# Attention in 64x64 quadrants (layers 2, 3) in place of three shared 128x1024 PSUM tiles (layer 0)

## The chip, the cores and the metric

The kernel runs on one core of a Trainium2 chip. The metric is the device time of one execution in microseconds, the median of the runs. Engines are named as the profile names them: PE (TensorE matmuls) with its weight loads (PEld), DVE (VectorE), ACT (ScalarE), POOL (GpSimd) and SP (the queue that issues most DMAs).

## What is computed

Four layers act in turn on x of shape (2, 512, 32, 32) in fp32. Layer 0 is attention on 64 sampled keys for 1024 queries, with a bias from a small MLP on every (query, key) pair, then a projection and a channel MLP. Layer 1 is a linear attention. Layers 2 and 3 are group norm, attention with 8 heads of 64 channels over 1024 positions, a projection and a residual. The parts that the change touches are these (cut from the reference):

```python
# layer 0: the bias of 16 (batch, group) units, 1024 queries x 64 keys each
bias = relu(bias @ cpb_w1 + cpb_b1)        # 2 -> 128
bias = relu(bias @ cpb_w2 + cpb_b2)        # 128 -> 128
bias = (bias @ cpb_w3 + cpb_b3)            # 128 -> 1
sim = einsum('bhid,bhjd->bhij', qh, kh) + bias
# layers 2 and 3
attn = softmax(einsum('bhcn,bhcm->bhnm', q, k) * scale)
out = einsum('bhnm,bhcm->bhcn', attn, v)
```

## The kernel before, in words

**Layer 0.** `layer0` (L99) builds, for each of 16 units u (one group of 64 channels of one image; two units are a pair), the bias of 64 keys. It does so in 16 quads per unit, written (o, jj): four keys by 1024 queries each. `first_hidden` (L368) lets DVE add a row `x` (tile `tx`) and a column `y` (tile `ty`, in PSUM) with a clamp at zero, into four tiles `h1`. `second_hidden` (L389) forms four PSUM tiles `hp` of 128x1024, for q from 0 to 3. Each takes 8 matmuls of 32 output columns (L400), four of them side by side in the four column strips of the array. ACT evacuates each `hp` with a Relu (L404) into a tile `h2`. After the first one ACT also multiplies by a sign `flip` (L411, only for q equal to 1, on the tile of q equal to 0), and POOL does the other sign (L408) and two adds (L412). `last_product` (L416) is then 8 matmuls `sim` per two quads (L427).

Weights: `last_weights` (L173) loads cpb_w3 as a row `w3row`, takes its absolute value and multiplies the columns of `l0w2` by it (L180 to L182), so that the Relu needs only a bias `magb`. `table` (L352) makes `tx` on POOL (L363) and `ty` on DVE (L365).

Around the quads, generators `offsets`, `sampled` and `attend` make the next pair's queries, sampling spots, keys and values, and finish the unit before. One step of them is taken between quads. They place small matmuls on PE, and work on ACT that shares its queue with the Relus: a Gelu after a convolution (L258), the logarithm of positions (L276 to L278), the absolute values `wx` and `w` (L315, L316), the Exp of a softmax (L461), copies (L239, L479).

PSUM in layer 0 (L123 to L125): one pool `c_ps_h` of three tiles of 128x1024 (two banks each) with one tag "ps" serves `hp` and all the small results, `c_ps_t` holds `ty` and `c_ps_s` holds `sim`: eight banks in all.

**Layers 2 and 3.** `heads_bounded` (L842) works through 16 units (b, p, h): image, pair of heads, half of the queries. Each has eight blocks n of 128 keys. A score block (L863) is two matmuls, of 64 rows by 128 columns, one for each head of the pair, into a tile `s` of two banks; ACT takes Exp into `e` (L871); DVE adds the eight `e` into `sum` (L875, L877). A value block (L888) is two matmuls of 128 rows by 64 columns that accumulate into `o`. After the eighth, two products of ones with `sum` (L899) give the denominators `d`, DVE takes the reciprocal (L901) and multiplies (L902). PE's order is written out by hand: two score blocks, then the two value blocks of two blocks before, and so on; the product of ones follows the last value block directly.

PE's order is by hand in both places (`manual_schedule`); the other engines' instructions are placed by a scheduler, and each engine works through its own queue in order. Every fp32 matmul appears in the profile as two instructions.

Of the kernel before, what the change touches and what calls it, by code (L numbers as in the profile page):

```python
# [11 lines left out]
F32 = mybir.dt.float32  # L12
# [6 lines left out]
P = 128  # L19
# [28 lines left out]
class Net:  # L48
# [50 lines left out]
    def layer0(self):  # L99
# [3 lines left out]
        with ExitStack() as ctx:  # L103
# [16 lines left out]
            self.hid2 = self.pool(ctx, "c_hid2", 11)  # L120
            self.soft = self.pool(ctx, "c_soft", 1)
            apool = self.pool(ctx, "c_att", 1)
            ps = self.ps_h = self.pool(ctx, "c_ps_h", 3, psum=True)  # L123
            self.ps_t = self.pool(ctx, "c_ps_t", 1, psum=True)
            ps_s = self.pool(ctx, "c_ps_s", 1, psum=True)  # L125

            with self.tc.manual_schedule(engines={mybir.EngineType.PE}):
                pairs = [{} for _ in range(BP)]
# [44 lines left out]
    def last_weights(self, keep):  # L173

        nc = self.nc
        row = keep.tile([P, P], F32, tag="row", name="w3row")
        nc.scalar.dma_start(row, self.io["cpb_w3"].partition_broadcast(P))  # L180
        nc.vector.scalar_tensor_tensor(row, row, -1.0, row, ALU.mult, ALU.max)
        nc.vector.tensor_tensor(self.l0w2, self.l0w2, row, ALU.mult)  # L182
        w3 = self.colr("w3r", 4)
        self.magb = keep.tile([P, 4], F32, tag="magb", name="magb")
        nc.vector.scalar_tensor_tensor(self.magb, w3, -1.0, w3, ALU.mult, ALU.max)
        nc.vector.tensor_tensor(self.magb, self.magb, self.colr("b2r", 4), ALU.mult)
        sign = keep.tile([P, 4], F32, tag="sign", name="sign")
        nc.vector.tensor_scalar(sign, w3, 0.0, 2.0, ALU.is_ge, ALU.mult)
        nc.vector.tensor_scalar(sign, sign, -1.0, None, ALU.add)
        self.flip = keep.tile([P, 2], F32, tag="flip", name="flip")  # L190
        self.ends = keep.tile([P, 2, 60], F32, tag="ends", name="ends")
        nc.vector.memset(self.ends, 0.0)
        for p in range(2):
            nc.vector.tensor_tensor(
                self.flip[:, p : p + 1], sign[:, 2 * p : 2 * p + 1], sign[:, 2 * p + 1 : 2 * p + 2], ALU.mult
            )
            for k in range(4):
                rows = slice(32 * k, 32 * k + 32)
                nc.vector.tensor_copy(self.ends[rows, p, 28 + k : 29 + k], sign[rows, 2 * p + 1 : 2 * p + 2])
# [152 lines left out]
    def table(self, u, c, pairs):  # L352

        nc = self.nc
        logs = pairs[u // 2]["logs"].rearrange("(a j c i) e -> a c j (i e)", a=2, j=2, c=4)
        got = self.lpool.tile([P, 2, 8, 2, W], F32, tag="logs", name=f"lb{u}{c}")
        nc.sync.dma_start(
            got.rearrange("p j i d x -> p j (i d x)"), logs[u % 2, c].unsqueeze(0).to_broadcast([P, 2, 16 * W])  # L360
        )
        x = self.tab.tile([P, 2, 8, W], F32, tag="x", name=f"tx{u}{c}")
        nc.gpsimd.tensor_scalar(x, got[:, :, :, 0, :], self.col("cpb_w1", 0), self.col("cpb_b1"), ALU.mult, ALU.add)  # L363
        y = self.ps_t.tile([P, 2, 8, W], F32, tag="y", name=f"ty{u}{c}")
        nc.vector.tensor_scalar(y, got[:, :, :, 1, :], self.col("cpb_w1", 1), None, ALU.mult)  # L365
        return x, y
# [22 lines left out]
    def second_hidden(self, u, o, jj, h1):  # L389


        nc = self.nc
        got, before = [], None
        for q in range(4):
            hp = self.ps_h.tile([P, N], F32, tag="ps", name=f"hp_{u}_{o}{jj}{q}")
            for h in range(2):
                cut = slice(h * HF, (h + 1) * HF)
                for k in range(4):
                    rows = slice(32 * k, 32 * k + 32)
                    nc.tensor.matmul(  # L400
                        hp[rows, cut], lhsT=self.l0w2[:, 32 * q : 32 * q + 32], rhs=h1[k][:, cut], start=True, stop=True
                    )
            y = self.hid2.tile([P, N], F32, tag="h2", name=f"h2_{u}_{o}{jj}{q}")
            nc.scalar.activation(y, hp, AF.Relu, bias=self.magb[:, q : q + 1])  # L404
            if q % 2 == 0:
                before = y
                if q == 2:
                    nc.gpsimd.tensor_scalar(y, y, self.flip[:, 1:2], 1.0, ALU.mult, ALU.mult)  # L408
            else:
                if q == 1:  # L410
                    nc.scalar.activation(before, before, AF.Copy, scale=self.flip[:, 0:1])  # L411
                nc.gpsimd.tensor_tensor(y, y, before, ALU.add)  # L412
                got.append(y)
        return got
# [427 lines left out]
    def heads_bounded(self, k, ones, data):  # L842

        nc = self.nc
        with ExitStack() as ctx:
            ep = self.pool(ctx, f"b{k}_e", 6)  # L850
            ap = self.pool(ctx, f"b{k}_a", 2)
            ps_s = self.pool(ctx, f"b{k}_ps_s", 2, psum=True)
            ps_o = self.pool(ctx, f"b{k}_ps_o", 2, psum=True)
            ps_d = self.pool(ctx, f"b{k}_ps_d", 2, psum=True)

            def score(unit, n):
                b, p, h, state = unit
                qs, ks, _ = data[b]
                cut = slice(h * HF, (h + 1) * HF)
                s = ps_s.tile([P, 2, HF], F32, tag="s", name=f"s{k}{b}{p}{h}{n}")  # L860
                for par in range(2):
                    rows = slice(par * DH, (par + 1) * DH)
                    nc.tensor.matmul(  # L863
                        s[:, par, :],
                        lhsT=ks[p][rows, n * P : (n + 1) * P],
                        rhs=qs[p][rows, cut],
                        start=True,
                        stop=True,
                    )
                e = ep.tile([P, 2, HF], F32, tag="e", name=f"e{k}{b}{p}{h}{n}")  # L870
                nc.scalar.activation(e, s, AF.Exp)  # L871
                state.setdefault("e", {})[n] = e
                if n == 1:
                    state["sum"] = ap.tile([P, 2, HF], F32, tag="sum", name=f"sum{k}{b}{p}{h}")
                    nc.vector.tensor_tensor(state["sum"], state["e"][0], e, ALU.add)  # L875
                elif n > 1:
                    nc.vector.tensor_tensor(state["sum"], state["sum"], e, ALU.add)  # L877

            def value(unit, n):
                b, p, h, state = unit  # L880
                v = data[b][2]
                if n == 0:
                    state["o"] = ps_o.tile([P, HF], F32, tag="o", name=f"o{k}{b}{p}{h}")
                e = state["e"].pop(n)
                for par in range(2):
                    rows = slice(par * DH, (par + 1) * DH)
                    at = (2 * p + par) * DH
                    nc.tensor.matmul(  # L888
                        state["o"][rows, :],
                        lhsT=v[:, n, at : at + DH],  # L890
                        rhs=e[:, par, :],
                        start=(n == 0),
                        stop=(n == NB - 1),
                    )
                if n == NB - 1:
                    d = ps_d.tile([P, HF], F32, tag="d", name=f"d{k}{b}{p}{h}")
                    for par in range(2):
                        rows = slice(par * DH, (par + 1) * DH)
                        nc.tensor.matmul(d[rows, :], lhsT=ones, rhs=state["sum"][:, par, :], start=True, stop=True)  # L899
                    r = ap.tile([P, HF], F32, tag="r", name=f"r{k}{b}{p}{h}")  # L900
                    nc.vector.reciprocal(r, d)  # L901
                    nc.vector.tensor_tensor(data[b][0][p][:, h * HF : (h + 1) * HF], state["o"], r, ALU.mult)  # L902

            units = [(b, p, h, {}) for b in range(B) for p in range(CT) for h in range(2)]
            steps = [(unit, n) for unit in units for n in range(NB)]
            with self.tc.manual_schedule(engines={mybir.EngineType.PE}):
                for i in range(0, len(steps) + 2, 2):
                    for unit, n in steps[i : i + 2]:
                        score(unit, n)
                    if i >= 2:  # L910
                        for unit, n in steps[i - 2 : i]:
                            value(unit, n)

    def heads_general(self, k, data):
        with ExitStack() as ctx:
# [131 lines left out]
def _layout(i):  # L1047
# [10 lines left out]
    def over(v):  # L1058
# [25 lines left out]
        "grid": _grid(),  # L1084
        "l0_qkv": np.stack([_pairs(a["qw"]), _pairs(a["kw"]), _pairs(a["vw"])], 1),
        "cpb_w2": a["cpb_w2"],
        "cpb_w3": a["cpb_w3"].reshape(P),
        "out_w": _blocks(a["out_w"]).transpose(1, 0, 2),
        "mlp_w1": _blocks(a["mlp_w1"]),
        "mlp_w2": _blocks(a["mlp_w2"]).reshape(CT, 4, P, C).transpose(0, 2, 1, 3),  # L1090
# [23 lines left out]
```

## Time and profile before

| what | value |
|---|---|
| median of 3 runs | 3788.34 us (3786.85 to 3789.77) |
| the profiled execution | 3789.77 us, its span 3787.8 us, granted clock 0.985 |
| start to the first `hp` | 0 to 42.2 us |
| layer 0 attention | 42.2 to 2289.7 us, PE busy 2174.2 of 2247.4 |
| layer 0 MLP | 2289.7 to 2730.2 us, PE busy 439.7 of 440.6 |
| layer 1 | 2730.2 to 2809.1 us |
| layer 2: norm, q, k, v | 2809.1 to 2976.8 us |
| layer 2: heads | 2976.8 to 3236.6 us, PE busy 256.0 of 259.7 |
| layer 2: projection; layer 3: norm | 3236.6 to 3297.2 us |
| layer 3: q, k, v | 3297.2 to 3468.3 us |
| layer 3: heads | 3468.3 to 3728.1 us, PE busy 256.0 of 259.8 |
| layer 3: projection, output | 3728.1 to 3787.8 us |

The stages are read from the view of busy times in stretches. A row of the groups gives line, engine, operation, tiles and shapes, then the count; after the bar come busy time in us, the mean ns of one, and the idle time of the engine before it with what ended most of it. A line of the timeline gives start and duration in us, engine, line and operation, with the idle time before it in brackets.

### The profile page before, as it was taken

To read this page: it belongs to the slowest core of one execution; us is meant where nothing else is said; L and a number is where in the kernel's file an instruction comes from. 1 tells how busy PE (TensorE), PEld (TensorE's weight loads), DVE (VectorE), ACT (ScalarE), POOL (GpSimd) and SP (SyncE) were. 2 spreads that over 40 slices of the span, in tenths; PEclk is the share of its full clock that TensorE was granted. 3 is DMA by queue.
4 is the path that set the end of the run, shared out by engine and by line. 5 is a ranking of instruction groups with operands and counts; after the bars stand their busy time and mean duration, and the time that the engine had idled before them with its cause. 6 is when DMAs were issued, how large, how long until landed. Compare 5 with 4: busy or idle time off the path is not lost.

```text
span 3787.8 us, 55147 instructions
## 1 busy us (share of the span) xinstructions
PE 3645.5 (96%) x24000; PEld 1273.4 (34%) x24000; DVE 2097.9 (55%) x2059; ACT 1842.8 (49%) x1831; POOL 1647.3 (43%) x917
## 2 busy tenths in 40 slices
PE   5999999999999999999999999999999999999999
PEld 2222233332322332332233324444554333343333
DVE  5767667767667567667666640000052577524774
ACT  4676676676676476676677651100010344102441
POOL 3677777776776576776777750000001000010000
PEclk8999999999999999999999999999999999999999
DMA  2000000000000000000100021000000000000001
GB/s 91 20 18 12 20 18 18 14 18 19 18 18 14 12 18 18 14 18 19 35 18 18 12 90 46 0 0 0 1 4 0 34 1 1 16 0 1 1 1 45
DMA packets 28610, 68.09 MB, mean 18 GB/s; under 512 B 4416, under 2 KB 6080, under 8 KB 27072
## 3 DMA queue, kind: packets, MB, share of 16 engines
q1 hardware_dynamic: 27488, 62.34, 5.7%
q8 instruction: 193, 3.16, 0.3%
q10 hardware_dynamic: 864, 2.06, 0.2%
q14 instruction: 65, 0.53, 0.0%
HBM read 59.92 MB, written 4.46 MB: 17 GB/s over the span
## 4 chain that ended last, share of the span: by engine, by line
PE 88%; DVE 6%; DMA 2%; ACT 2%; issue 1%; POOL 0%; ACTq 0%; SPq 0%; DVEq 0%; POOLq 0%
PE hp L400 42%; PE s L863 6%; PE o L888 6%; PE m L528 6%; PE m L537 6%; PE sim L427 5%; PE qk0p L757 3%; PE pb L494 3%; PE qk1p L757 3%; PE vp L798 3%; DVE prod L243 2%; DVE h L378 2%; PE out_b L494 1%; ACT h L404 1%; DVE conv L256 1%
## 5 line engine op out<-in xcount | busy, mean ns | idle before, releaser
L400 PE MATMUL hp<-h,w 128*32 128x512 f32 x16384 | 1816.2, 598 | 77.1 <-ACT h L404 50.1
L378 DVE CUSTOM_DVE_ANT_1 h<-tx,ty 128x1024 f32<-128x1024 f32 x1024 | 1187.3, 1213 | 646.7 <-PE hp L400 646.3
L412 POOL TENSOR_TENSOR h<-h,h 128x1024 f32<-128x1024 f32 x512 | 1224.9, 2393 | 592.0 <-ACT h L404 571.2
L404 ACT ACTIVATE h<-hp,magb 128x1024 f32<-128x1024 f32 x1024 | 1133.3, 1111 | 587.9 <-PE hp L400 524.2
L400 PEld LDWEIGHTS hp<-h,w 128*32 128x32 f32 x16384 | 525.0, 111 | 1306.6 <-issue 1189.5
L871 ACT ACTIVATE e<-s 128x1024 f32<-128x1024 f32 x256 | 248.3, 1023 | 255.3 <-PE s L863 255.2
L408 POOL TENSOR_SCALAR h<-h,flip 128x1024 f32<-128x1024 f32 x256 | 300.0, 1172 | 4.3 <-ACT h L404 4.3
L411 ACT ACTIVATE h<-h,flip 128x1024 f32<-128x1024 f32 x256 | 294.4, 1150 | 7.9
L771 POOL TENSOR_TENSOR sq<-q 128x1024 f32<-128x1024 f32 x16 | 30.3, 1892 | 555.3 <-DVE q L765 555.3
L863 PE MATMUL s<-q,k 64*128 64x512 f32 x1024 | 254.5, 615 | 5.1 <-ACT e L871 3.4
L877 DVE TENSOR_TENSOR sum<-sum,e 128x1024 f32<-128x1024 f32 x192 | 233.0, 1213 | 41.1 <-ACT e L871 30.9
L427 PE MATMUL sim<-h,ends 128*32 128x512 f32 x2048 | 245.9, 595 | 2.5 <-POOL h L412 2.5
L888 PE MATMUL o<-e,v 128*64 128x512 f32 x1024 | 247.5, 605 | 0.0
L528 PE MATMUL m<-mx,w 128*128 128x512 f32 x512 | 220.5, 592 | 0.8 <-DVE x L498 0.8
L537 PE MATMUL m<-mh,w 128*128 128x512 f32 x512 | 220.4, 592 | 0.0
L568 POOL MEMSET l1ones<- 128x128 f32 x1 | 0.2, 205 | 483.6 <-PE m L537 483.6
L532 ACT ACTIVATE mh<-m,cols 128x512 f32<-128x512 f32 x64 | 44.1, 688 | 336.4 <-PE m L528 336.4
L545 DVE SCALAR_TENSOR_TENSOR x<-m,cols,x 128x512 f32<-128x512 f32 x16 | 12.0, 749 | 318.0 <-PE m L537 318.0
L863 PEld LDWEIGHTS s<-q,k 64*128 64x128 f32 x1024 | 88.1, 186 | 169.4 <-issue 86.9
L769 ACT ACTIVATE k<-qk1p,cols 128x512 f32<-128x512 f32 x32 | 22.0, 689 | 243.1 <-PE qk1p L757 243.1
L528 PEld LDWEIGHTS m<-mx,w 128*128 128x128 f32 x512 | 97.2, 190 | 123.6 <-issue 122.0
L537 PEld LDWEIGHTS m<-mh,w 128*128 128x128 f32 x512 | 97.3, 190 | 122.5 <-issue 122.5
(173 smaller groups left out, 2128.8 us busy)
## 6 DMA issues: line engine op xcount, KB each, us to landing
lb<-logs SPq DMA_DIRECT2D x64, 512.0 KB, 4.9
w<-in_mlp_w SPq DMA_DIRECT2D x8, 1024.0 KB, 11.9
qkv<-in_l_qkv SPq DMA_DIRECT2D x8, 768.0 KB, 6.9
x<-in_x SPq DMA_DIRECT2D x8, 512.0 KB, 7.8
out<-x SPq DMA_DIRECT2D x8, 512.0 KB, 2.6
proj<-in_l_proj SPq DMA_DIRECT2D x8, 256.0 KB, 6.1
l1w<-in_l_w SPq DMA_DIRECT2D x1, 1280.0 KB, 7.0
ow<-in_out_w ACTq DMA_DIRECT2D x1, 1024.0 KB, 12.5
```

What stands on the lines that cost most here:

```text
L378: self.nc.vector._custom_dve(TENSOR_ADD_SAT, out=h[:, k, :, :], in0=x[:, jj, i + k, :].unsqueeze(1).to_broadcast([P, H, W]), in1=y[:, jj, ...
L400: nc.tensor.matmul(hp[rows, cut], lhsT=self.l0w2[:, 32 * q : 32 * q + 32], rhs=h1[k][:, cut], start=True, stop=True)
L404: nc.scalar.activation(y, hp, AF.Relu, bias=self.magb[:, q : q + 1])
L408: nc.gpsimd.tensor_scalar(y, y, self.flip[:, 1:2], 1.0, ALU.mult, ALU.mult)
L411: nc.scalar.activation(before, before, AF.Copy, scale=self.flip[:, 0:1])
L412: nc.gpsimd.tensor_tensor(y, y, before, ALU.add)
L427: nc.tensor.matmul(sims[u][at : at + 32, :], lhsT=self.ends[:, p, 28 - 4 * o : 60 - 4 * o], rhs=z[jj][p][:, h * HF : (h + 1) * HF], start= ...
L528: nc.tensor.matmul(acc, lhsT=w1[t][:, o * P : (o + 1) * P], rhs=xn[t], start=(t == 0), stop=(t == CT - 1))
L537: nc.tensor.matmul(acc, lhsT=w2[t // 4][:, t % 4, o * P : (o + 1) * P], rhs=hs[t], start=(t == 0), stop=(t == nh - 1),)
L863: nc.tensor.matmul(s[:, par, :], lhsT=ks[p][rows, n * P : (n + 1) * P], rhs=qs[p][rows, cut], start=True, stop=True,)
L871: nc.scalar.activation(e, s, AF.Exp)
L888: nc.tensor.matmul(state["o"][rows, :], lhsT=v[:, n, at : at + DH], rhs=e[:, par, :], start=(n == 0), stop=(n == NB - 1),)
```

## The change

Two edits are made together.

In layer 0 the three shared PSUM tiles are given up: `hp` has a pool of two tiles of its own, and the small results have a pool `c_ps` of two tiles of one bank. The absolute value of cpb_w3 is no longer multiplied into `l0w2`; the Relu takes it as a scale `mag` for each partition. The load of `w3row` and two DVE instructions go. `tx` is made on DVE in place of POOL.

In layers 2 and 3 every matmul of the heads is 64 rows by 64 columns. A score block is four matmuls (two heads by two halves of the keys), a value block four (two halves of the keys by two heads); the value's halves of keys go to two banks, `o[:, 0]` and `o[:, 1]`, which ACT and DVE add (copy, then add). The product of ones is done the same way. The sum of the `e` is split: POOL adds blocks 0, 1, 3, 5 into `some`, DVE blocks 2, 4, 6, 7 into `sum`, and DVE adds `some` to it. `ps_o` has one buffer for each of `o` and `d`. The order on PE is one score block, then one value block of two blocks before, but a unit's value blocks 0 and 1 both follow its score block 3, and the product of ones of the unit before follows in step 4.

```diff
-            ps = self.ps_h = self.pool(ctx, "c_ps_h", 3, psum=True)
+            self.ps_h = self.pool(ctx, "c_ps_h", 2, psum=True)
             self.ps_t = self.pool(ctx, "c_ps_t", 1, psum=True)
             ps_s = self.pool(ctx, "c_ps_s", 1, psum=True)
+            ps = self.pool(ctx, "c_ps", 2, psum=True)
...
-        row = keep.tile([P, P], F32, tag="row", name="w3row")
-        nc.scalar.dma_start(row, self.io["cpb_w3"].partition_broadcast(P))
-        nc.vector.scalar_tensor_tensor(row, row, -1.0, row, ALU.mult, ALU.max)
-        nc.vector.tensor_tensor(self.l0w2, self.l0w2, row, ALU.mult)
+        self.mag = keep.tile([P, 4], F32, tag="mag", name="mag")
+        nc.vector.scalar_tensor_tensor(self.mag, w3, -1.0, w3, ALU.mult, ALU.max)
...
-        nc.gpsimd.tensor_scalar(x, got[:, :, :, 0, :], self.col("cpb_w1", 0), self.col("cpb_b1"), ALU.mult, ALU.add)
+        nc.vector.tensor_scalar(x, got[:, :, :, 0, :], self.col("cpb_w1", 0), self.col("cpb_b1"), ALU.mult, ALU.add)
...
-            hp = self.ps_h.tile([P, N], F32, tag="ps", name=f"hp_{u}_{o}{jj}{q}")
+            hp = self.ps_h.tile([P, N], F32, tag="hp", name=f"hp_{u}_{o}{jj}{q}")
...
-            nc.scalar.activation(y, hp, AF.Relu, bias=self.magb[:, q : q + 1])
+            nc.scalar.activation(y, hp, AF.Relu, bias=self.magb[:, q : q + 1], scale=self.mag[:, q : q + 1])
...
-            ps_o = self.pool(ctx, f"b{k}_ps_o", 2, psum=True)
-            ps_d = self.pool(ctx, f"b{k}_ps_d", 2, psum=True)
+            ps_o = self.pool(ctx, f"b{k}_ps_o", 1, psum=True)
...
-                for par in range(2):
-                    rows = slice(par * DH, (par + 1) * DH)
-                    nc.tensor.matmul(s[:, par, :], lhsT=ks[p][rows, n * P : (n + 1) * P], rhs=qs[p][rows, cut], start=True, stop=True)
+                for par, rows in enumerate(halves):
+                    for c in range(2):
+                        at = n * P + c * DH
+                        nc.tensor.matmul(s[halves[c], par, :], lhsT=ks[p][rows, at : at + DH], rhs=qs[p][rows, cut], start=True, stop=True)
...
+                for r, rows in enumerate(halves):
+                    for par in range(2):
+                        at = (2 * p + par) * DH
+                        nc.tensor.matmul(o[halves[par], r, :], lhsT=v[rows, n, at : at + DH], rhs=e[rows, par, :], start=(n == 0), stop=(n == NB - 1))
                 if n == NB - 1:
+                    res = data[b][0][p][:, h * HF : (h + 1) * HF]
+                    nc.scalar.copy(res, o[:, 0, :])
+                    nc.vector.tensor_tensor(res, o[:, 1, :], res, ALU.add)
...
+            def divide(unit):
+                d = ps_o.tile([P, 2, HF], F32, tag="d", name=f"d{k}{b}{p}{h}")
+                for r, rows in enumerate(halves):
                     for par in range(2):
+                        nc.tensor.matmul(d[halves[par], r, :], lhsT=ones[rows, :], rhs=state["sum"][rows, par, :], start=True, stop=True)
+                nc.scalar.copy(t, d[:, 0, :])
+                nc.vector.tensor_tensor(t, d[:, 1, :], t, ALU.add)
+                nc.vector.reciprocal(t, t)
+                nc.vector.tensor_tensor(res, res, t, ALU.mult)
...
+                for i in range(len(steps) + 5):
+                    if i < len(steps):
+                        score(*steps[i])
+                    for j in ([], [i - 3, i - 2])[i % NB == 3] if i % NB in (2, 3) else [i - 2]:
+                        if 0 <= j < len(steps):
+                            value(*steps[j])
+                    if i % NB == 4 and i > NB:
+                        divide(steps[i - NB][0])
```

## The prediction

> **What bounds the kernel now.** I read the view of busy times by stage first: PE is busy 3645.5 of 3787.8 us, in layer 0's attention 2174.2 of 2247.4 and in each heads stage 256.0 of 259.7. The end is set by PE, so each stage is asked two things: what PE's own stream costs, and where it waits. The timeline of an undisturbed quad of layer 0 (a quad with jj = 1, starting at 279.35) answers for layer 0.
>
> ```profile
> 279.35 13.92 PE L400 MATMUL hp<-h,w 128*32 128x512 f32 x128
> ...
> 281.38 1.12 ACT L404 ACTIVATE h<-hp,magb 128x1024 f32<-128x1024 f32 x1 [2.35 <-PE hp L400]
> ...
> 282.53 1.15 ACT L411 ACTIVATE h<-h,flip 128x1024 f32<-128x1024 f32 x1
> ...
> 283.58 2.34 ACT L404 ACTIVATE h<-hp,magb 128x1024 f32<-128x1024 f32 x2
> ...
> 286.55 1.12 ACT L404 ACTIVATE h<-hp,magb 128x1024 f32<-128x1024 f32 x1 [0.63 <-PE hp L400]
> ...
> 288.18 1.12 ACT L404 ACTIVATE h<-hp,magb 128x1024 f32<-128x1024 f32 x1 [0.51 <-PE hp L400]
> ...
> 293.08 1.90 PE L427 MATMUL sim<-h,ends 128*32 128x512 f32 x16
> ```
>
> 128 hp instructions are eight tiles, two quads: 293.08 - 279.35 = 13.73 us, 1.717 a tile, with no gap. The flip (L411) stands between the first and the second Relu, so the second starts only at 283.58, though its tile was complete about 0.5 us earlier. With three PSUM tiles nobody cares. Where ACT is held up longer, PE does stop; next is the worst place, a Gelu that waits for a convolution with Relus queued behind it.
>
> ```profile
> 352.57 0.35 ACT L258 ACTIVATE ge<-conv,cols 128x64 f32<-128x64 f32 x1 [7.53 <-DVE conv L256]
> 352.83 1.10 ACT L404 ACTIVATE h<-hp,magb 128x1024 f32<-128x1024 f32 x1
> ...
> 353.98 12.50 PE L400 MATMUL hp<-h,w 128*32 128x512 f32 x96 [5.57 <-ACT h L404]
> ```
>
> PE resumes 0.05 us after the Relu's end (352.83 + 1.10): the handshake that I use below. The heads' timeline:
>
> ```profile
> 3022.04 0.20 PEld L888 LDWEIGHTS o<-e,v 128*64 128x64 f32 x4 [0.76 <-issue]
> 3022.04 1.94 PE L888 MATMUL o<-e,v 128*64 128x512 f32 x8
> ...
> 3023.91 0.30 PEld L863 LDWEIGHTS s<-q,k 64*128 64x128 f32 x4 [0.81 <-ACT e L871]
> 3023.91 1.99 PE L863 MATMUL s<-q,k 64*128 64x512 f32 x8
> 3024.44 0.19 PEld L863 LDWEIGHTS s<-q,k 64*128 64x128 f32 x2 [0.24 <-issue]
> ...
> 3028.67 3.36 DVE L901 RECIPROCAL r<-d 128x512 f32<-128x512 f32 x1 [0.39 <-PE d L899]
> ```
>
> Within a run of scores the weight loads follow after 0.24 us, at each change of tile shape only after 0.76 to 0.81. A round (two score and two value blocks) lasts from 3020.12 to 3023.91, 3.79 us. Four blocks at array speed are 4 x 0.858 = 3.43 (0.858 is half of 1.717: 8 instructions, full array). ACT (1.02 us of 1.9 a block) isn't the bound.
>
> [...] pairs of rows (s) and of columns (o) each reach full speed. [...] one such step (L309, a subtraction) takes 1.23 us at 35.17 with POOL idle, and 2.50 at 401.35 beside a POOL add. [...] After the 5.57 us gap four groups of weight loads come 0.86 us apart in place of 0.43.
>
> **The change, part by part.**
>
> Layer 0, undisturbed quads. With two tiles, hp 3 waits for Relu 1. In the jj = 1 quad Relu 1 ends at 283.58 + 1.12 = 284.70, PE could start at 284.75, its slot was 279.35 + 3 x 1.717 = 284.50: **0.25 us late**. In the jj = 0 quad (start 286.22) the same sum gives 290.39 + 1.12 + 0.05 - 291.37 = 0.19. hp 2 waits for Relu 0 (282.50 + 0.05, slot 282.78): free by 0.23. The next quad's first two tiles wait for Relus 2 and 3, both 0.2 us or more in time. Restarting costs about 0.02 (128 instructions from 54.73 to 68.48 after a wait, 13.75). Mean 0.24 us a quad. Some 28 of 256 quads have worse waits, so 228 x 0.24 = **+54 us**. Nothing hides it: PE is the bound.
>
> Layer 0, disturbed quads, by walking one pair (326 to 410 us) and its odd unit with the new queue order. The Gelu: `tx` now stands before the convolution on DVE, +0.6 (0.5 to 0.75), and hp 3 behind the Exp and its table load (1.28), +0.75. The logarithm with its table load keeps Relu 1 until 392.8, hp 3 +2.3. In the new order `wx` and `w`, which wait for the spots' DMA and DVE, precede Relu 3: that ends at about 400.6 while hp 1 of the next quad was due at 396.3, +4.4. Gone are 3.0 us (405.99) where transposes held tiles, and 0.6 behind the attention copies. Odd units: Exp and table load delay Relu 1, 2.1 against 0.3 now (496.45), +1.7. In all 0.6 + 0.75 + 2.3 + 4.4 - 3.6 + 1.7 = 6.1, seven pairs: **+42 us**, between 0 (if stalls overlap) and 60 (clock drops added).
>
> `w3row`'s load and two DVE steps go: DVE starts the products at 17.41, the copies that it needs end at 14.21, -3.1. Two `tx` and one more wait come before the first h on DVE, +1.1. **-2 us.** Later `tx` are hidden in DVE's idle time (4.6 of 7.7 us busy a quad); without it, 64 x 0.75 = 48. POOL loses 60 us of work that nobody waited for. The Relu's scale operand isn't in the trace: I take 0; a twentieth of a microsecond more would add directly to each stall (+12), and I see no reason for a gain. The avg DMA moves ahead of the spots on SP at the start, 0.3 us of issue before its data exist: nothing.
>
> Heads. A unit is 17 blocks of 0.858 = 14.59 us if four quadrants run at once; now it is 16.00 (3028.55 to 3044.55): -1.41, all of it mode changes. New wait: `o` has one buffer, so value block 0 waits for ACT's copy and DVE's add. From the unit's start: last value block of the unit before ends at 3.43, copy at 3.9 to 4.5 (behind an Exp of 1.02; the copy as L479, 0.58), add to 5.2; PE wants to start at 5.15. DVE arrives there late: reciprocal 11.05 to 14.41, multiply to 15.1, three chained adds of 1.29 (the 3.87 of three at 3033.62) to 19.0, that is 4.4 in the next unit. So the add is just in time, +0.1, and any POOL contention is paid in full: I take +0.4 (bounds 0.1 and 3.7, see the rivals). POOL's adds (2.39) end 3 us before `some` is needed. `e` has six buffers, the latest reader is DVE's add four blocks on: no wait. Queued behind the copy on ACT is the next Exp, which has 1 us to spare. Net -1.01 x 32 = **-32 us**. At each end the product of ones waits for the sum until 4.4 where PE is through at 1.7: **+5 us** for both layers; the reciprocal behind it lies beside the projection as now.
>
> Sum: 54 + 42 - 2 - 32 + 5 = **+67 us** on the span of 3787.8 us (the profiled execution 3789.77, 1.4 above the median), so 3788 + 67 = **3855 us**.
>
> **Rivals.** (A) Faster: the pool of their own for small results pays as much as the third tile did. PE's waits in layer 0 on Relus are 50.1 us in the profile; if they vanished, and ACT's queue kept Relu 1 in time, layer 0 would cost 0 to -10: 3788 - 8 - 27 = **3753**. It decides at Relu 1 ending 0.25 us earlier. Against it: the flip stays ahead of Relu 1 in the new order. (B) The quadrants run two at a time: 17 x 0.858 more for each of 32 units, +467, **about 4320**. Against it: pairs in either direction overlap today. (C) DVE and POOL contend in the heads: three adds at 2.4 in place of 1.29, value block 0 is 3.7 late, +105: **about 3960**. For it: 2.50 against 1.23 above; against: by my times POOL is done before DVE's adds begin. (D) Layer 0's disturbed quads cost nothing more: **3813**.
>
> **How the numbers follow.** Forecast 0.58; D 0.20; A 0.09; C 0.10; B 0.03. A measurement here tells about 0.2% (7.6 us) from no change. Slower is forecast, B, C and most of D: 0.87; same 0.04; faster 0.09. The range starts below D at 3802 (steady stalls a little smaller) and goes to 3915 (clock drops +18, scale +12, half of a mild C +30); outside are A, B and the heavy part of C.
>
> **What would show it.** Right: PE waits on the Relu (now 50.1 us for hp) near 130, of them over 200 of about 0.2 us; hp waits in the quads of log and w; rounds of heads of 14.6 to 15.2 us a unit, weight loads of s and o without the 0.8 us gaps. Wrong: undisturbed quads still 15.45 us a pair of quads, or a heads stage over 250 us.

## The result and the profile after

The changed kernel takes 3893.8 us (median; 3893.6 to 3895.4), the kernel before in the same session 3788.7 us. The ratio is 1.028, 95% interval 1.026 to 1.030: 105 us slower, where 67 were forecast. The profiled execution has a span of 3892.0 us, 104.2 more than that of before. The view of busy times by stage tells where they are. Two of its lines after, layer 0 and the heads of layer 2 (stretch, length, then busy time of PE, PEld, DVE, ACT and POOL, the granted clock, DMA), and the table of all:

```profile
40.09:2863.70 2823.61, 2677.41 (x20312) 839.28 (x20313) 1629.01 (x1497) 1618.40 (x1492) 1524.82 (x802) 0.98 0.06 18
3110.61:3352.98 242.37, 236.27 (x2176) 81.41 (x2177) 161.17 (x127) 147.69 (x161) 113.62 (x48) 0.99 0.03 12
```

| stage | before, us | after, us | difference |
|---|---|---|---|
| start to the first `hp` | 42.2 | 40.1 | -2.1 |
| layer 0 attention and MLP | 2688.0 | 2823.6 | +135.6 |
| layer 1; norm, q, k, v of layer 2 | 246.6 | 246.9 | +0.3 |
| heads, layer 2 | 259.7 | 242.4 | -17.4 |
| heads, layer 3 | 259.8 | 242.6 | -17.2 |
| projection of layer 2; norm, q, k, v of layer 3 | 231.7 | 235.3 | +3.5 |
| last projection, output | 59.7 | 61.2 | +1.5 |

**Layer 0, the steady part.** First three rows of the groups after, the range of `tx` (nanoseconds: least, median, most), and a line of the view of waits (total, times, longest); behind them the Relu's row and the same wait in the kernel before.

```profile
L397 PE MATMUL hp<-h,w 128*32 128x512 f32 x16384 | 1881.1, 604 | 151.8 <-ACT h L401 135.6 <-DVE h L375 16.0
...
L401 ACT ACTIVATE h<-hp,magb,mag 128x1024 f32<-128x1024 f32 x1024 | 1215.7, 1201 | 658.9 <-PE hp L397 631.5 <-POOL h L409 26.9 <-issue 0.2
...
L360 DVE TENSOR_SCALAR tx<-lb,cols 128x512 f32<-128x512 f32 x64 | 151.2, 2362 | 0.4 <-DMA lb<-logs 0.3
L360 DVE TENSOR_SCALAR tx<-lb,cols x64: 515/2661/2673, 36.9 to 2304.3; 128x512 f32<-128x512 f32 x64
```

```profile
PE hp L397 <- ACT h L401: 135.6, 259, 5.6
```

```profile
L404 ACT ACTIVATE h<-hp,magb 128x1024 f32<-128x1024 f32 x1024 | 1133.3, 1111 | 587.9 <-PE hp L400 524.2 <-POOL qpad L234 19.3 <-POOL h L412 15.3
```

```profile
PE hp L400 <- ACT h L404: 50.1, 17, 5.6
```

PE waits for a Relu 259 times in place of 17; there are 256 quads. (That these waits add up to 135.6 us, as layer 0's difference does, is a coincidence: before there were 50.1.) The Relu itself, with its scale operand, takes 1201 ns in place of 1111. `tx` on DVE takes 2362 ns on average where 750 were assumed, and the average hides two kinds: 55 of the 64 run beside an addition on POOL and take 2.65 to 2.67 us, nine run while POOL rests, or begin before its addition does, and take 0.52 to 0.55. The timeline of two undisturbed quads, from one product `sim` to the next; two lines of the kernel before, then the kernel after:

```profile
277.63 1.90 PE L427 MATMUL sim<-h,ends 128*32 128x512 f32 x16
...
293.08 1.90 PE L427 MATMUL sim<-h,ends 128*32 128x512 f32 x16
```

```profile
270.54 1.90 PE L424 MATMUL sim<-h,ends 128*32 128x512 f32 x16
...
272.25 5.33 PE L397 MATMUL hp<-h,w 128*32 128x512 f32 x48
...
274.28 1.21 ACT L401 ACTIVATE h<-hp,magb,mag 128x1024 f32<-128x1024 f32 x1 [2.26 <-PE hp L397]
275.52 1.15 ACT L408 ACTIVATE h<-h,flip 128x1024 f32<-128x1024 f32 x1
276.58 2.34 ACT L401 ACTIVATE h<-hp,magb,mag 128x1024 f32<-128x1024 f32 x2
277.82 7.07 PE L397 MATMUL hp<-h,w 128*32 128x512 f32 x64 [0.23 <-ACT h L401]
...
285.06 1.92 PE L397 MATMUL hp<-h,w 128*32 128x512 f32 x16 [0.17 <-ACT h L401]
...
286.81 1.90 PE L424 MATMUL sim<-h,ends 128*32 128x512 f32 x16
```

After three tiles (48 instructions) PE stops, and goes on when Relu 1, behind Relu 0 and the flip, is over. Two quads take 286.81 - 270.54 = 16.27 us, before 293.08 - 277.63 = 15.45: 0.41 lost a quad. The brackets show only 0.17 and 0.23, because the instructions' modelled ends lie over the rest (a line of 48 has 5.33 us, where three tiles at 1.717 are 5.15). The distance between the same product in two rounds is the safe reading.

Taken so, 93 of the 126 rounds from one product `sim` to the next are longer by 0.8 us than the same rounds before, 76 us together. (Most of these rounds hold other small products too, and lose the same.) The other 33 differ by between -4 and +9 us, 65 together; behind the last product layer 0 is 6 us shorter than before.

**Layer 0, disturbed quads.** Five PE lines of the timeline after, in the places that the prediction walked: the Gelu, the Exp with its table load (1.28 us), the logarithm, `wx` and `w`, and the Exp of an odd unit.

```profile
366.39 3.23 PE L397 MATMUL hp<-h,w 128*32 128x512 f32 x16 [5.55 <-ACT h L401]
370.61 7.07 PE L397 MATMUL hp<-h,w 128*32 128x512 f32 x64 [0.99 <-ACT h L401]
...
407.65 3.64 PE L397 MATMUL hp<-h,w 128*32 128x512 f32 x32 [1.93 <-ACT h L401]
...
414.89 8.00 PE L397 MATMUL hp<-h,w 128*32 128x512 f32 x48 [3.60 <-ACT h L401]
...
518.71 8.77 PE L397 MATMUL hp<-h,w 128*32 128x512 f32 x64 [2.03 <-ACT h L401]
```

The gap is in the brackets, and what follows it tells of the clock: 64 instructions take 7.07 us at full speed, 8.77 after the odd unit's gap; 48 take 5.33 elsewhere, 8.00 after the gap of 3.60.

**Heads.** Timeline after, one unit's turn; the product of ones `d` marks the period.

```profile
3148.01 1.04 PE L908 MATMUL d<-sum,ones 64*64 64x512 f32 x8
...
3157.45 1.90 PE L862 MATMUL s<-q,k 64*64 64x512 f32 x16
...
3157.85 0.58 ACT L900 COPY q<-o 128x512 f32<-128x512 f32 x1
...
3158.46 0.69 DVE L901 TENSOR_TENSOR q<-o,q 128x512 f32<-128x512 f32 x1
...
3159.21 0.21 PEld L891 LDWEIGHTS o<-e,v 64*64 64x64 f32 x8 [0.74 <-DVE q L901]
...
3162.69 1.04 PE L908 MATMUL d<-sum,ones 64*64 64x512 f32 x8
```

A unit takes 3162.69 - 3148.01 = 14.68 us, before 16.00 by the same products:

```profile
3027.59 1.03 PE L899 MATMUL d<-sum,ones 128*64 128x512 f32 x4
...
3043.59 1.03 PE L899 MATMUL d<-sum,ones 128*64 128x512 f32 x4
```

The 14.68 are 0.09 above the 14.59 of 17 blocks at array speed. Value block 0 waits for DVE's add of `o`, which ends at 3159.15; PE goes on at 3159.21, less than a tenth late. The end of a heads stage, and the granted clock (the first number after the colon pair is the length, the last but two the clock) in two stretches behind it:

```profile
3349.07 1.98 PE L908 MATMUL d<-sum,ones 64*64 64x512 f32 x8 [2.47 <-DVE sum L880]
```

```profile
3349.00:3353.00 4.00, 2.00 (x9) 0.35 (x9) 1.84 (x4) 0.59 (x1) 0.00 (x0) 0.50 0.09 23
3353.00:3357.00 4.00, 4.00 (x5) 1.78 (x6) 3.51 (x2) 1.28 (x1) 0.00 (x0) 0.50 0.03 8
```

The last product of ones waits 2.47 us for the sum, as forecast, and then runs at half clock (1.98 us in place of 1.04 for eight instructions). The projection's first matmuls do so too: its 128 take 58.23 us in place of 55.17 in layer 2, 56.55 in layer 3. Before, the clock was 1.00 at this place.

### The profile page after: what moved, and what is told of

Its sections match the earlier page's. It is cut to its first block, busy times and chain, and to the rows that moved or that the text cites. A ratio compares the mean times of both kernels' runs of the same rounds, so it can differ in the third digit from the quotient of the medians.

```text
span 3892.0 us, 59463 instructions
## 1 busy us (share of the span) xinstructions
PE 3674.9 (94%) x26176; PEld 1255.1 (32%) x26176; DVE 2160.8 (56%) x2089; ACT 1970.3 (51%) x1895; POOL 1818.3 (47%) x949
## 4 chain that ended last, share of the span: by engine, by line
PE 67%; ACT 19%; DVE 7%; issue 4%; DMA 2%; POOL 0%; ACTq 0%; SPq 0%; DVEq 0%
PE hp L397 23%; ACT h L401 14%; PE m L525 6%; PE m L534 6%; PE s L862 5%; PE o L891 5%; PE sim L424 5%; ACT h L408 5%; PE pb L491 3%; PE qk0p L754 3%; PE qk1p L754 3%; PE vp L795 2%; DVE h L375 2%; DVE prod L240 2%; PE out_b L491 1%
## 5 line engine op out<-in xcount | busy, mean ns | idle before, releaser
L397 PE MATMUL hp<-h,w 128*32 128x512 f32 x16384 | 1881.1, 604 | 151.8 <-ACT h L401 135.6
L401 ACT ACTIVATE h<-hp,magb,mag 128x1024 f32<-128x1024 f32 x1024 | 1215.7, 1201 | 658.9 <-PE hp L397 631.5
L397 PEld LDWEIGHTS hp<-h,w 128*32 128x32 f32 x16384 | 502.0, 111 | 1468.5 <-issue 818.1
L866 ACT ACTIVATE e<-s 128x1024 f32<-128x1024 f32 x256 | 258.6, 1024 | 152.8 <-PE s L862 152.8
L862 PE MATMUL s<-q,k 64*64 64x512 f32 x2048 | 259.9, 590 | 5.1 <-ACT e L866 3.4
L891 PE MATMUL o<-e,v 64*64 64x512 f32 x2048 | 260.8, 592 | 0.0
L873 POOL TENSOR_TENSOR some<-some,e 128x1024 f32<-128x1024 f32 x64 | 151.3, 2364 | 82.5 <-ACT e L866 80.2
L871 POOL TENSOR_TENSOR some<-e,e 128x1024 f32<-128x1024 f32 x32 | 75.9, 2371 | 212.5 <-ACT q L900 139.1
L360 DVE TENSOR_SCALAR tx<-lb,cols 128x512 f32<-128x512 f32 x64 | 151.2, 2362 | 0.4 <-DMA lb<-logs 0.3
```

What stands on the lines that cost most here:

```text
L397: nc.tensor.matmul(hp[rows, cut], lhsT=self.l0w2[:, 32 * q : 32 * q + 32], rhs=h1[k][:, cut], start=True, stop=True)
L862: nc.tensor.matmul(s[halves[c], par, :], lhsT=ks[p][rows, at : at + DH], rhs=qs[p][rows, cut], start=True, stop=True)
L891: nc.tensor.matmul(o[halves[par], r, :], lhsT=v[rows, n, at : at + DH], rhs=e[rows, par, :], start=(n == 0), stop=(n == NB - 1),)
```

## The experiments

My theory: layer 0 loses because hp 3 waits for Relu 0, flip and Relu 1 in a row, and the scale operand lengthens that row; the heads gain because with tiles of one shape the gaps of 0.76 to 0.81 us before the weight loads go. The rivals are that two tiles are too few in any order, that `tx` on DVE is the cause, and that the heads gain by their order. The kernel before was run beside the versions in three sessions, with medians of 3789.3, 3791.7 and 3790.0 us; a few microseconds between runs of different sessions tell little.

**The heads alone.** The kernel before with the new `heads_bounded`.

> The kernel before with the new heads of layers 2 and 3 alone; layer 0 as before. Theory (the two halves of the change are independent; the heads gained 17.3 us a layer by the two profiles): 3788.7 - 34.6 = 3754 us, each heads stage 242.5 us. Rival (the heads gain in the profile came from what layer 0 left behind, the clock or the order of loads): between 3765 and 3789.

Measured: 3760.0 us (3751.4 to 3764.1), ratio 0.992 (0.990 to 0.995). The two heads stages take the 242 us of the changed kernel. The 6 us by which 3754 was missed are near the two slow starts of the projection (+3.5 and +1.5 in the table above), which I had not counted in; they are also within the spread of this run's own executions. So this half of the change is a gain of some 29 us.

**Layer 0 alone.** The changed kernel with the old `heads_bounded`.

> The changed kernel with the old heads of layers 2 and 3; only layer 0 is changed. Theory (independent halves): 3893.8 + 34.6 = 3928 us, two undisturbed quads of layer 0 16.27 us. Rival (the parts interact): off 3928 by more than 8.

Measured: 3925.0 us (3923.1 to 3927.6), ratio 1.036 (1.034 to 1.039). The parts add up: 3760.0 + 3925.0 - 3789.3 = 3895.7, and 3893.8 is what both together take.

**No scale operand.**

```
+        row = keep.tile([P, P], F32, tag="row", name="w3row")
+        nc.scalar.dma_start(row, self.io["cpb_w3"].partition_broadcast(P))
+        nc.vector.scalar_tensor_tensor(row, row, -1.0, row, ALU.mult, ALU.max)
+        nc.vector.tensor_tensor(self.l0w2, self.l0w2, row, ALU.mult)
...
-            nc.scalar.activation(y, hp, AF.Relu, bias=self.magb[:, q : q + 1], scale=self.mag[:, q : q + 1])
+            nc.scalar.activation(y, hp, AF.Relu, bias=self.magb[:, q : q + 1])
```

> The changed kernel with |w3| folded back into the weights, so that the Relu has no scale operand. Theory (hp 3 waits for Relu 0, flip, Relu 1 in a row, and the operand makes both Relus 0.09 us longer): the Relu back at 1.11 us, stall 0.41 - 0.18 = 0.23 us a quad, two quads 15.9 us, 256 x 0.18 = 46 less and 2 more at the start: 3850 us. Rival 1 (the operand counts once a stall): 3873. Rival 2 (the Relu is longer for another reason, such as the tile's place in PSUM): 3892 to 3896.

Measured: 3833.9 us (3831.7 to 3835.4), ratio 1.012 (1.010 to 1.014), 60 less than the changed kernel. The group of the Relu, then two undisturbed quads, then the odd unit's gap:

```profile
L405 ACT ACTIVATE h<-hp,magb 128x1024 f32<-128x1024 f32 x1024 | 1132.8, 1109 | 674.5 <-PE hp L401 614.8 <-POOL h L413 29.2
```

```profile
272.84 1.90 PE L428 MATMUL sim<-h,ends 128*32 128x512 f32 x16
274.55 14.36 PE L401 MATMUL hp<-h,w 128*32 128x512 f32 x128
288.73 1.90 PE L428 MATMUL sim<-h,ends 128*32 128x512 f32 x16
...
514.35 8.99 PE L401 MATMUL hp<-h,w 128*32 128x512 f32 x80 [1.84 <-ACT h L405]
```

Two quads take 15.89 us: the stall is (15.89 - 15.45) / 2 = 0.22 a quad, and the operand adds 0.19, two Relus by 0.09. If every round gains as much, that makes 128 x (16.27 - 15.89) = 49 us. Of the other 11, some 10 are in the odd units: the gap is 1.84 in place of 2.03, and no half clock follows (80 instructions in 8.99, where full speed gives 8.78 and the steady stall of one quad 0.22), so that two quads there take 18.42 us in place of 20.48 in six of the seven. So a gap that is 0.19 us shorter saves 8.77 - 7.07 = 1.70 us of half clock behind it; the last section shows what the falls of the clock go with. Both rivals fall, and the time is 16 us under the 3850 expected. Here PE's stall is so short that the view of waits no longer shows it (36 waits on the Relu in place of 259); the distances do.

**The flip on POOL.**

```
             if q % 2 == 0:
                 before = y
-                if q == 2:
-                    nc.gpsimd.tensor_scalar(y, y, self.flip[:, 1:2], 1.0, ALU.mult, ALU.mult)
+                nc.gpsimd.tensor_scalar(y, y, self.flip[:, q // 2 : q // 2 + 1], 1.0, ALU.mult, ALU.mult)
             else:
-                if q == 1:
-                    nc.scalar.activation(before, before, AF.Copy, scale=self.flip[:, 0:1])
```

> The changed kernel with the first flip of a quad on POOL, as the second one is, so that nothing stands between Relu 0 and Relu 1 on ACT. Theory (the flip is what makes Relu 1 late, not the two tiles by themselves): no stall in undisturbed quads, two quads 15.45 us, 256 x 0.41 = 104 less, and up to 15 less in disturbed quads: 3775 to 3790 us. Rival 1 (two tiles are too few in any order, PE waits for each tile's release): two quads stay over 16 us, 3880 or more. Rival 2 (POOL, at 2 x 2.39 + 2 x 1.15 = 7.1 us of 7.7 a quad, becomes the bound and holds z and the buffers): 3800 to 3860, PE waits on POOL.

Measured: 3772.9 us (3771.1 to 3774.5), ratio 0.996 (0.995 to 0.997): 121 less than the changed kernel. It is under the kernel before too, but by the gain of the heads: the heads alone reach 3760.0. Two quads in its timeline:

```profile
267.63 1.90 PE L421 MATMUL sim<-h,ends 128*32 128x512 f32 x16
269.34 13.92 PE L397 MATMUL hp<-h,w 128*32 128x512 f32 x128
283.08 1.90 PE L421 MATMUL sim<-h,ends 128*32 128x512 f32 x16
```

128 instructions in one piece, 15.45 us for two quads, with the longer Relu still there. In undisturbed quads two tiles are enough as long as nothing stands between two Relus on ACT; the flip's place is the cause of the steady loss. POOL doesn't become the bound: PE waits for it once, 2.3 us, as before (2.5).

**Three tiles again.** `hp` and the small results share one pool of three; operand and `tx` stay as changed.

```
-            self.ps_h = self.pool(ctx, "c_ps_h", 2, psum=True)
+            ps = self.ps_h = self.pool(ctx, "c_ps_h", 3, psum=True)
...
-            ps = self.pool(ctx, "c_ps", 2, psum=True)
```

> The changed kernel with hp and the small results in one pool of three tiles again; the scale operand, tx on DVE and the missing w3row stay as changed. Theory (a third tile gives hp 3 a slot of 1.717 us more, which swallows the 0.41 us, so the longer Relu and tx are free there): two quads 15.45 us, 3750 to 3765 us, as with the new heads alone (3760). Rival (the operand or tx costs by itself, whatever the tiles): 3775 or more, up to 3850 if all of 1024 x 0.09 us counted.

Measured: 3776.8 us (3771.8 to 3784.9), ratio 0.996 (0.995 to 0.997). The undisturbed quads are back at 15.45 us, as the theory says, but the time is the rival's lower end: operand and `tx` cost some 17 us above the 3760 of the heads alone even with three tiles. In the traces they are in disturbed quads. The gaps at the Gelu are 5.79 to 5.95 us in six pairs; with the heads alone, where operand and `tx` are as before, they are 5.53 to 5.54 in two pairs and 3.41 to 3.63 in four, which is 10 us less. But in the kernel before, with the same layer 0, they are 5.54 to 5.58 in five pairs and 3.61 in one, so these gaps aren't the same in two traces of one layer 0. Which of the two edits does how much of it here was not separated.

**`tx` on POOL again.**

```
-        nc.vector.tensor_scalar(x, got[:, :, :, 0, :], self.col("cpb_w1", 0), self.col("cpb_b1"), ALU.mult, ALU.add)
+        nc.gpsimd.tensor_scalar(x, got[:, :, :, 0, :], self.col("cpb_w1", 0), self.col("cpb_b1"), ALU.mult, ALU.add)
```

> The changed kernel with tx on POOL again. Theory (2.36 us on DVE beside POOL's adds, but DVE idles longer than that in each quad): 3886 to 3896 us. Rival (tx late on DVE delays h and so PE, or the Gelu by 0.6 us): below 3880.

Measured: 3875.3 us (3875.1 to 3875.7), ratio 1.022 (1.018 to 1.025): 18.5 less, so the rival is right about the sign. Undisturbed quads stay at 16.26; the difference is mostly in two kinds of disturbed ones. Where the logarithm and `w` fall, two quads take 24.8 to 25.0 us in five pairs, in place of 26.1 to 26.4 in four of them and 25.2 in one. In the odd units the gap is unchanged, but the clock mostly is not halved after it:

```profile
515.57 7.07 PE L397 MATMUL hp<-h,w 128*32 128x512 f32 x64 [2.02 <-ACT h L401]
```

This stands against 518.71 of the changed kernel: the same gap, 7.07 us in place of 8.77. Five of seven such gaps of this run have full speed behind them, in the changed kernel one of seven. This is 7 of the 18.5 us, and it comes from where the gaps fall, not from their length (last section).

**The pools alone.** No operand, `tx` on POOL, two pools of two tiles, the new heads.

> Of layer 0's change the two pools alone (two tiles for hp, two for the small results): |w3| folded into the weights, no scale operand, tx on POOL; the new heads. Theory (the split alone costs the stall without the scale, 0.22 us a quad, 256 x 0.22 = 57 above the 3760 of the new heads alone, and little in disturbed quads; tx on DVE was worth 10 to 18): 3810 to 3828 us. Rival (tx on DVE costs only with the scale operand, since it was the half clock after the 2.03 us gap, and that gap is 1.84 without the operand): 3829 to 3836.

Measured: 3828.3 us (3826.5 to 3831.9), ratio 1.010 (1.009 to 1.012). Between the two expectations: without the operand `tx` is worth 5.6 us, inside the two intervals, so the rival's reason (it costs mostly through the half clock after the odd unit's gap) is supported and not proved. The split itself costs 3828.3 - 3760.0 = 68 us. In the trace 93 rounds are longer by 0.45 us than with the heads alone, 42 us together; the rest is in the others.

**Two and two with all moved to POOL.** Two pools, no operand, flips and `tx` on POOL.

> The two pools of two tiles, no scale operand, both flips and tx on POOL, the new heads. Theory (with the flip off ACT two tiles are enough in undisturbed quads; the operand and tx cost only in disturbed ones, together 10 to 25 us of the 3773 with the flip on POOL): 3748 to 3765 us, at or a little below the new heads alone. Rival (POOL at 7.1 us of 7.7 a quad and tx on top gets behind and holds z): 3773 or more.

Measured: 3768.2 us (3765.8 to 3769.8), ratio 0.994 (0.993 to 0.996), 3 above the expected range and under the rival's. No wait of PE on POOL is new, so POOL isn't the bound; what stays are waits on the Relu in disturbed quads (61.0 us in 33 times). A pool of its own for small results doesn't beat the third tile.

**The flip on POOL with three tiles.** The kernel before with the flip moved and the new heads.

> Layer 0 of the kernel before, three tiles in one pool, with the first flip on POOL as well; the new heads. Theory (ACT has 1.15 us less a quad, so in disturbed quads it catches up sooner; the waits on ACT there, 48 us for hp in the run with the new heads alone, fall by a fifth to a third): 3742 to 3755 us. Rival (those waits are the Gelu's, the logarithm's and the Abs of w, not the flip's): 3756 to 3765.

Measured: 3760.2 us (3754.5 to 3763.4), ratio 0.992 (0.990 to 0.993). The rival's: nothing is gained over the heads alone.

```profile
PE hp L400 <- ACT h L404: 61.5, 21, 6.3
```

The waits on the Relu are not fewer (48.5 us in the run with the heads alone). With three tiles the flip is off the path. What on ACT the disturbed quads wait for in its place was not separated.

**Value products in tiles of 128 rows.** Scores in quadrants, values not.

```
-                for r, rows in enumerate(halves):
-                    for par in range(2):
...
+                for par in range(2):
+                    at = (2 * p + par) * DH
+                    nc.tensor.matmul(
+                        o[halves[par], 0, :],
+                        lhsT=v[:, n, at : at + DH],
+                        rhs=e[:, par, :],
...
-                    nc.scalar.copy(res, o[:, 0, :])
-                    nc.vector.tensor_tensor(res, o[:, 1, :], res, ALU.add)
+                    nc.vector.tensor_copy(res, o[:, 0, :])
```

> The changed kernel with the value products of the heads in tiles of 128 rows again (one accumulator, no add of halves), scores and product of ones in quadrants, order as changed. Theory (each change of tile shape costs 0.18 us, from (3.79 - 3.43) / 2 of the rounds before; about 14 changes a unit): 32 x 14 x 0.18 = 81 more, 3955 to 3995 us, and gaps of 0.8 us before the weight loads of s and o again. Rival (the gain came from the order and the shorter DVE work): 3888 to 3898.

Measured: 3955.1 us (3952.3 to 3957.9), ratio 1.042 (1.039 to 1.046): 61 more. The weight loads in its timeline, and the period of `d`:

```profile
3203.97 0.15 PEld L862 LDWEIGHTS s<-q,k 64*64 64x64 f32 x4 [0.28 <-issue]
3204.93 0.20 PEld L890 LDWEIGHTS o<-e,v 128*64 128x64 f32 x4 [0.81 <-issue]
3205.94 0.21 PEld L862 LDWEIGHTS s<-q,k 64*64 64x64 f32 x8 [0.81 <-issue]
```

```profile
3203.06 1.09 PE L906 MATMUL d<-sum,ones 64*64 64x512 f32 x8
...
3219.83 1.09 PE L906 MATMUL d<-sum,ones 64*64 64x512 f32 x8
```

0.81 us before each load at a change of shape, 0.28 without one, as before the change. A unit takes 16.77 us; (16.77 - 14.59) / 14 = 0.16 a change, somewhat under the 0.18 expected. (The run also drops the add of halves and copies `o` on DVE in place of ACT; what these do by themselves was not measured.) The theory holds, the size was 20 us too high.

**The plain order.**

```
-                    for j in ([], [i - 3, i - 2])[i % NB == 3] if i % NB in (2, 3) else [i - 2]:
-                        if 0 <= j < len(steps):
-                            value(*steps[j])
-                    if i % NB == 4 and i > NB:
+                    if 0 <= i - 2 < len(steps):
+                        value(*steps[i - 2])
+                    if i % NB == 1 and i > NB:
```

> The changed kernel with the heads in quadrants but every value block two blocks behind its score block, and the product of ones right after a unit's last value block. Theory (the order is there to cover the sum and the two copies of o: the sum ends at 3158.34 and the last value block at 3157.45 in the trace, so d waits 0.9 us a unit, and it saves the wait of 0.1): 32 x 0.8 = 26 more, 3905 to 3935 us. Rival 1 (the tile shape alone brings the gain): 3890 to 3898. Rival 2 (o and its one buffer wait as well): over 3940.

Measured: 3902.6 us (3894.5 to 3903.1), ratio 1.028 (1.025 to 1.031): about 9 more, between the two expectations. The intervals of the two ratios overlap; the length of a unit in the trace decides.

```profile
3217.03 1.23 DVE L880 TENSOR_TENSOR sum<-sum,some 128x1024 f32<-128x1024 f32 x1
...
3218.31 1.09 PE L908 MATMUL d<-sum,ones 64*64 64x512 f32 x8 [0.21 <-DVE sum L880]
```

The product of ones does wait for the sum in every unit, but DVE's queue moved with the order and the sum comes earlier than I took it: a unit is 15.03 us (3203.28 to 3218.31), 0.35 more than in the changed kernel and 0.97 less than before. So of the gain of 1.32 a unit, 0.97 come with the tile shape and the sum split between POOL and DVE, which were not taken apart, and 0.35 with the order.

## Why the prediction was right or wrong

- **Direction and mechanism: right.** PE's waits on the Relu for hp were to be near 130 us with over 200 short ones; they are 135.6 in 259. That the sums agree is partly luck: the forecast counted 0.24 a quad, and the view shows some 0.2 of the 0.41 that a quad really loses. The forecast of 67 us was 38 short, inside the range.
- **Undisturbed quads, +54: the mechanism is right, the size was not.** The stall was put at 0.24; it is 0.22 without the scale operand and 0.41 with it. The step that failed is "The Relu's scale operand isn't in the trace: I take 0". It costs 0.09 us an instruction, and a stall has two of them in its row (Relu 0 and Relu 1), not one as the +12 for a twentieth of a microsecond assumed. The runs show the price (1201 ns against 1109 to 1111), and at 0.09 a Relu two in each of 256 quads make 2 x 0.09 x 256 = 46 us. Operand and the half clock that follows it are 60 us, more than the whole miss.
- **Disturbed quads, +42: close, partly by offsetting errors.** Taking the 228 quads that the prediction counts, at 0.41, out of 135.6 leaves 42. The count isn't measured: by rounds, 93 with the steady loss make 76 us and all the rest of layer 0 makes 60. Of the single terms, hp 3 behind the Exp is 0.99 (0.75 said), the logarithm 1.93 (2.3), `wx` and `w` 3.60 (4.4), the odd unit 2.03 (2.1); the 3.02 of the transposes are gone. The Gelu's +0.6 didn't come (5.55 against 5.57), and the 0.6 behind the attention copies was not freed: the offsets' product now waits 0.67 there. The half clock after the gaps, only in the range, stands in their place.
- **The start, -2:** -2.1.
- **`tx` "hidden in DVE's idle time": wrong.** It takes 2.66 us beside POOL's adds, not 0.75, and costs 18.5 us with the operand, all in disturbed quads; without the operand some 6. DVE's mean idle time said nothing of the quads in which DVE is late. How much `tx` loses the trace shows, 0.52 us with POOL at rest against 2.66 beside its adds; the cause was not shown.
- **Heads, -32 and +5: the mechanism is right, the sum partly by luck.** A unit is 14.68 where 15.0 was said, so the 32 units give -42, ten more than forecast. The wait of value block 0 is 0.09 at most, the just-in-time sum without the +0.3 put on for contention: POOL's last add ends at 3153.50, DVE's last three begin at 3154.46 and take 1.23 to 1.28 us each, so rival C has no footing. The waits at the two ends are 2 x 2.47 = 4.9, but the half clock behind them was not foreseen: 3.06 + 1.38 us in the two projections and 0.9 in each last product, 6 in all. Net, by the table of stages, -34.6 in the heads and +5.0 behind them, -29.6 where -27 was said: two misses of opposite sign.
- **Rivals.** B (quadrants two at a time) falls: 17 blocks in 14.68 us. D falls with the gaps above. A falls as it was put, since the flip did stay ahead of Relu 1; but it was right about where it decides: with the flip away the same two pools give 3772.9 us.

The best of the versions is the simplest: the layer 0 of before with the new heads, 3760.0 us, 0.8% under the kernel before. Moving the flip as well makes no difference to that.

## What to carry to other kernels

Before taking a buffer away from a pipelined pair of engines, write down everything that stands in the consumer's queue between two uses of it, and price an operand added to the consumer once for each of its instructions in that row. Moving one foreign instruction out of that row was worth as much here (121 us) as the third buffer (117), and twice the operand (60). An engine's mean idle time hides nothing in the rounds where it is late: price a moved step there, beside the neighbours it will have, and look at the fastest and slowest of its instructions, not at their mean.

## What the runs showed of the hardware

- A scale per partition on a Relu of 128x1024 out of PSUM costs 0.09 us: 1.201 against 1.111, and 1.109 when it was taken away again.
- A DVE step from SBUF to SBUF with one tensor input (`tx`, 128x512) takes 2.65 to 2.67 us beside POOL's two-input adds and 0.52 to 0.55 while POOL rests. Its neighbour `ty`, which reads the same tile and writes PSUM, isn't slowed by POOL's `tx`: in the kernel before, 63 of 64 run beside it for most of their time, and all take 0.73 to 0.77. Beside an add it stands for at most 0.41 of its time, in the kernel after, where all take 0.73 to 0.78. The POOL adds of layer 0 stay at 2.39 us on average, before and after.
- Four tiles of 64x64 run at full array speed in fp32: in the kernel after, eight such instructions follow each other every 0.86 us (`s` at 3148.87, `o` at 3149.73, `s` at 3150.59), where eight of hp, with the full array, take 0.858. Pairs reach it too, in the kernel before: two weight loads every 0.43 us (`s` at 3020.66 and 3021.09, `o` at 3018.74 and 3019.17). A change between 64x64 and 128x64 costs 0.16 us, estimated from the 16.77 us of a unit above.
- Gaps of the same length have different effects on PE's clock: after gaps of 2.02 and 2.03 us 64 instructions take 8.77 us in some places, 7.07 in others. What differs is where the gap falls. In the traces of before and after the granted clock changes only at points of a grid of 3.41 us. First the gap before 518.71 of the changed kernel, then the one before 515.57 with `tx` on POOL, each by stretches of that grid:

```profile
515.84:519.25 3.41, 1.38 (x16) 0.25 (x12) 1.58 (x3) 3.40 (x5) 0.52 (x1) 1.00 0.00 0
519.25:522.67 3.42, 3.42 (x24) 0.89 (x20) 0.79 (x1) 1.17 (x2) 2.94 (x2) 0.50 0.00 0
```

```profile
511.44:514.86 3.42, 2.11 (x20) 0.52 (x16) 1.81 (x4) 3.39 (x5) 0.00 (x0) 1.00 0.00 0
514.86:518.27 3.41, 2.70 (x28) 0.91 (x32) 0.95 (x2) 2.37 (x3) 2.68 (x2) 1.00 0.00 0
518.27:521.68 3.41, 3.41 (x40) 1.01 (x36) 3.41 (x4) 2.95 (x4) 3.19 (x2) 1.00 0.00 0
```

The first gap lies within one stretch, PE is idle for 2.03 of 3.41 us, and the next stretch has half the clock. The second is cut in two by a point of the grid, 1.31 and 0.71 us, and the clock stays. In the changed kernel too, the one of the seven gaps that has full speed behind it, 2.03 us before 227.16, is cut by a point of the grid, 0.57 and 1.46 us; the six others are each within one stretch. Counted in the traces of before and after, behind the first 60 us and without the last stretch of each: all 35 stretches of full clock in which PE is idle for 2.0 us or more are followed by half clock; of the 2114 others three are, with 0.77 to 1.86 us idle. So in these two traces idle time under 2.0 us in a stretch nearly always left the clock alone, and what a gap of a little more did hung on its place. What sets the clock was not shown.
